# Four graph-attention layers on one core: the row factors G spread over the partitions by DMA and ScalarE in place of TensorE transposes

## The chip, the core and the metric

The kernel runs on one core of a Trainium2 chip. The metric is the device time of one launch in microseconds (us), the median of three runs. A core has a matrix engine (TensorE, in the profile PE for its matmuls and PEld for its weight loads), a vector engine (VectorE, DVE), a scalar engine (ScalarE, ACT), a general engine (GpSimd, POOL), and SyncE (SP), which here issues DMAs alone. The program emits one stream of instructions for each of them, and the streams wait for one another by semaphores. SBUF is the working memory, with 128 partitions; PSUM is the memory that the matmuls write to.

## The reference

Input: 16 graphs `x[b]` of 1024 nodes with 256 features, and one adjacency matrix `adj` (1024 x 1024) for all. Four layers run one after the other, each adding its result to `x`. Layers 0 and 2 have four heads of 64 features, layers 1 and 3 have one head of 256. Cut to what matters:

```
h = max(layernorm(x), 0)
q = h @ W                          # split into heads of D features
e[i,j] = leaky(a_src·q[i] + a_dst·q[j], slope)
e[i,j] = -inf where adj[i,j] == 0
x = x + act(softmax_j(e) @ q)      # act: elu in layers 0 to 2, relu in layer 3
```

Softmax is not changed by a factor that depends on i alone. The kernel uses this: up to such a factor, exp(leaky(s_i + d_j)) is exp(slope·d_j) times max(G_i, R_j), where G_i = exp(-(1-slope)·s_i) and R_j = exp((1-slope)·d_j), both with constants for safety. So the weight for head h is `w[j,i] = max(G[i], R[j]) * mask[j,i]`, with j on the partitions and i along the free axis. R is one number per partition. G varies along the free axis, so it has to stand as a row of 1024 numbers, the same in all 128 partitions. How it gets there is what the change is about.

## The kernel before

The work is cut into 64 **steps**, one for each pair of a graph and a layer. Four graphs (streams) are under way at a time, and the steps rotate over them (`order_of_steps`), so that a step's graph was last worked on four steps earlier in the steady part; in the first steps it is less. In the steady part four-head and one-head steps mostly alternate; steps 0 to 8 and the last three are irregular. The nodes are cut into C = 8 chunks of 128.

A step n has three parts.

**Preparation** (`preparation`, 17 pieces) gives layer norm statistics on VectorE (`bn`, L160; `mv`, L161), the reciprocal root on GpSimd (`rstd`, L164 and L165), the normalised tile `t` on GpSimd (L171, two halves of four instructions), transposes of it on TensorE (L179) that ScalarE takes out of PSUM with a relu (`hT`, L180), the projection on TensorE (L191) that ScalarE evacuates (`whx`, `sd`, L193 to L197), and last the `factors`: `rcol` (R, L203) and `gcol` (G, L206) on ScalarE, and a minimum on GpSimd (L208). `rcol` and `gcol` have a node on each partition. The PSUM tile `pp` (two buffers) serves transposes and projections.

**Aggregation** has 8 groups, k = 0 to 7. In a four-head step a head takes two groups, in a one-head step the head takes all eight. A group is a run of matmuls (`acc`, L243, two PSUM buffers) and one ScalarE evacuation (`y`, L247). Before it, `broadcast` (L217) makes the row G of a head in a PSUM tile `g` of 4 KB per partition (two buffers): eight TensorE transposes of a column of `gcol` that is repeated to 128 columns (L221). Then `weights` (L224) makes eight tiles `w` of 128 x 1024 on VectorE (L227); the tiles stand in a ring of `WBUFS` = 21 buffers.

**Finish** (`finish`) divides (`r`, L264; `y`, L268), takes the elu with GpSimd (L273), ScalarE (L274) and VectorE (L280), and adds into `x` on GpSimd (L281); in layer 3 it adds on VectorE (L283), stores with a DMA on SP (L284) and loads the next graph (L146).

The order in which everything is emitted is written out by hand, under `tc.manual_schedule()` (L349). For each group k of step n the loop emits: the `w` tiles that the group needs and that are still missing, the group's matmuls and its evacuation, pieces of the finish of step n-1 (at k = 0, 1, 2, 3), up to 4 (four heads) or 2 (one head) further `w` tiles with the `broadcast` that they need, and last the pieces of preparation that are due. The preparation of step n+2 is planned at group 0 of step n (for a few early steps and the last ones at group 4), and `PREPARATION` gives each piece's distance from there in groups: statistics at 0 and 1, `t` at 1, the first transposes at 3, the factors at 9. A `broadcast` can only be emitted once its step's last piece of preparation has been (`done["prepared"]`). In steps that are planned late, this makes the `broadcast` of the next step's first head come after group 6.

Of the kernel before, what the change touches and what calls it, by code (L numbers as in the profile page):

```python
# [24 lines left out]
F32 = mybir.dt.float32  # L25
# [3 lines left out]
AF = mybir.ActivationFunctionType  # L29
# [4 lines left out]
P = 128  # L34
# [1 line left out]
SHIFT = 60.0  # L36
EXP_SHIFT = math.exp(SHIFT)
STREAMS = 4
WBUFS = 21
PREPARATION = (0, 1, 1, 1, 3, 3, 4, 4, 5, 5, 6, 6, 7, 7, 8, 8, 9)  # L40


LAYERS = [
# [8 lines left out]
def kernel(ctx: ExitStack, tc: tile.TileContext, x, adj, ws, avs, out):  # L52
    nc = tc.nc
    B, N, F = x.shape
    C = N // P
# [5 lines left out]
    ident = const.tile([P, P], F32, name="ident")  # L61
# [17 lines left out]
    with tc.tile_pool(name="wprep", bufs=2) as wp, tc.tile_pool(  # L79
        name="wpsum", bufs=2, space=PSUM  # L80
    ) as wps:
        for l, (H, slope, hs, _) in enumerate(LAYERS):
# [3 lines left out]
            for part in range(2):  # L86
                nc.scalar.dma_start(
                    out=a_bc[:, part],
                    in_=bass.AP(tensor=avs[l].tensor, offset=avs[l].offset + part * D,
                                ap=[[0, P], [hs, H], [1, D]]),  # L90
# [24 lines left out]
    with tc.tile_pool(name="mprep", bufs=2) as mp, tc.tile_pool(  # L115
        name="mpsum", bufs=2, space=PSUM
# [16 lines left out]
    small = ctx.enter_context(tc.tile_pool(name="small", bufs=4))  # L133
    work = ctx.enter_context(tc.tile_pool(name="work", bufs=2))
    ps_g = ctx.enter_context(tc.tile_pool(name="ps_g", bufs=2, space=PSUM))
    ps_acc = ctx.enter_context(tc.tile_pool(name="ps_acc", bufs=2, space=PSUM))
    ps_p = ctx.enter_context(tc.tile_pool(name="ps_p", bufs=2, space=PSUM))

    L = len(LAYERS)
# [2 lines left out]
    state = [dict() for _ in steps]  # L142
# [5 lines left out]
    def preparation(n):  # L148

        b, l = steps[n]  # L150
        H, slope, _, _ = LAYERS[l]
        D = F // H
        st = state[n]

        def stats(half):
            if half == 0:
                st["mv"] = small.tile([P, C, 2], F32, name="mv")
                st["bn"] = small.tile([P, C, 6], F32, name="bn")
            for c in range(half * HALF, (half + 1) * HALF):
                nc.vector.bn_stats(st["bn"][:, c, :], xs[b][:, c, :])  # L160
                nc.vector.bn_aggr(st["mv"][:, c, :], st["bn"][:, c, :])  # L161
            if half == 1:
                rstd = st["rstd"] = small.tile([P, C], F32, name="rstd")
                nc.gpsimd.tensor_scalar(rstd, st["mv"][:, :, 1], EPS, None, op0=ALU.add)  # L164
                nc.gpsimd.tensor_tensor(rstd, rstd, neghalf, op=ALU.pow)  # L165

        def normalise(half):
            xn = st["xn", half] = prep.tile([P, HALF, F], F32, name="t4", bufs=3)
            for q in range(HALF):
                c = half * HALF + q  # L170
                nc.gpsimd.tensor_scalar(xn[:, q, :], xs[b][:, c, :], st["mv"][:, c, 0:1],  # L171
                                        st["rstd"][:, c:c + 1], op0=ALU.subtract, op1=ALU.mult)

        def transpose(half, k):
            if k == 0:
                st["hT", half] = prep.tile([P, K, HALF * P], F32, name="hT")
            pt = ps_p.tile([P, HALF, P], F32, name="pp")
            for q in range(HALF):
                nc.tensor.transpose(pt[:, q, :], st["xn", half][:, q, k * P:(k + 1) * P], ident)  # L179
            nc.scalar.activation(st["hT", half][:, k, :], pt.rearrange("p q i -> p (q i)"),  # L180
                                 AF.Relu)

        def project(c):
            if c == 0:
                st["whx"] = prep.tile([P, C, H, D + 1], F32, name="whx", bufs=3)
                st["sd"] = small.tile([P, C, 2 * H], F32, name="sd")
            whx = st["whx"]
            half, q = divmod(c, HALF)
            pw = ps_p.tile([P, F + 2 * H], F32, name="pp")
            for k in range(K):  # L190
                nc.tensor.matmul(pw, lhsT=st["hT", half][:, k, q * P:(q + 1) * P],  # L191
                                 rhs=wx[l][:, k, :], start=(k == 0), stop=(k == K - 1))
            nc.scalar.activation(whx[:, c, :, D], pw[:, F + H:F + 2 * H], AF.Exp, bias=nbias[l],  # L193
                                 scale=slope)
            nc.scalar.activation(st["sd"][:, c, :], pw[:, F:F + 2 * H], AF.Copy)
            for h in range(H):
                nc.scalar.activation(whx[:, c, h, 0:D], pw[:, h * D:(h + 1) * D], AF.Copy,  # L197
                                     scale=whx[:, c, h, D:D + 1])

        def factors():  # L200
            sd = st["sd"]
            rcol = st["rcol"] = small.tile([P, C, H], F32, name="rcol")
            nc.scalar.activation(rcol, sd[:, :, H:2 * H], AF.Exp, bias=rbias[l],  # L203
                                 scale=1.0 - slope)
            gcol = st["gcol"] = small.tile([P, C, H], F32, name="gcol")
            nc.scalar.activation(gcol, sd[:, :, 0:H], AF.Exp, bias=rbias[l],  # L206
                                 scale=-(1.0 - slope))
            nc.gpsimd.tensor_scalar(gcol, gcol, EXP_SHIFT, None, op0=ALU.min)  # L208

        out = [lambda: stats(0), lambda: stats(1), lambda: normalise(0), lambda: normalise(1)]  # L210
        for half in range(2):
            out += [lambda half=half, k=k: transpose(half, k) for k in range(K)]
            out += [lambda c=c: project(c) for c in range(half * HALF, (half + 1) * HALF)]

        return list(zip(PREPARATION, out + [factors], strict=True))

    def broadcast(n, h):  # L217

        g = state[n]["g", h] = ps_g.tile([P, N], F32, name="g")
        for c in range(C):  # L220
            nc.tensor.transpose(g[:, c * P:(c + 1) * P],  # L221
                                state[n]["gcol"][:, c, h:h + 1].to_broadcast([P, P]), ident)

    def weights(n, h, jc):  # L224

        w = state[n]["w", h, jc] = work.tile([P, N], F32, name="w", bufs=WBUFS)
        nc.vector.scalar_tensor_tensor(w, state[n]["g", h], state[n]["rcol"][:, jc, h:h + 1],  # L227
                                       masks[LAYERS[steps[n][1]][3]][:, jc, :],
                                       op0=ALU.max, op1=ALU.mult)
# [66 lines left out]
    def groups(n):  # L296
        if LAYERS[steps[n][1]][0] == 1:
# [3 lines left out]
    tiles = [(n, h, jc) for n, (b, l) in enumerate(steps) for h in range(LAYERS[l][0])  # L301
             for jc in range(C)]
    place = {t: i for i, t in enumerate(tiles)}
    done = {"tiles": 0, "g": 0, "free": 0, "prepared": 0, "wanted": 0}
    agenda = []

    def prepare(upto):

        while agenda and (agenda[0][0] <= upto or agenda[0][1] < done["wanted"]):
            _, n, piece, last = agenda.pop(0)  # L310
            piece()
            if last:
                done["prepared"] = n + 1

    def plan(n, at):
        new = preparation(n)
        agenda.extend((at + k, n, piece, i == len(new) - 1) for i, (k, piece) in enumerate(new))
        agenda.sort(key=lambda a: a[:2])

    def emit_tiles(upto, must=False):  # L320
        while done["tiles"] < min(upto, len(tiles)):
            i = done["tiles"]

            while done["g"] <= min(i + C // 2, len(tiles) - 1):
                n, h, _ = tiles[done["g"]]
                if n >= done["prepared"]:
                    if i < done["g"] or not must:
                        break
                    done["wanted"] = n + 1
                    prepare(-1)  # L330
                broadcast(n, h)
                done["g"] += C
            if i >= done["g"]:
                return
            weights(*tiles[i])
            done["tiles"] += 1
# [8 lines left out]
    for n in range(2):  # L345
        plan(n, -99)
        prepare(0)
    ending = []
    with tc.manual_schedule():  # L349
        for n in range(len(steps)):  # L350
            for k, (h, i0, per) in enumerate(groups(n)):
# [9 lines left out]
                ahead = 4 if per > 1 else 2  # L361
                emit_tiles(min(done["tiles"] + ahead, done["free"] + WBUFS))
                prepare(8 * n + k)
# [43 lines left out]
```

## Time and profile before

| what | value |
|---|---|
| runs | 2884.19, 2884.19, 2882.7 us; median 2884.19 |
| profiled execution, own time | 2886.49 us |
| its span, first to last instruction | 2884.7 us |
| mean granted TensorE clock | 0.986 |
| PE / DVE / ACT / POOL busy, share of the span | 94% / 69% / 33% / 48% |
| transposes that make G (L221) | 1280 of 277 ns, 171.9 us busy |
| `w` tiles (L227) | 1280 of 1271 ns, 1541.9 us busy |
| ScalarE, one 128 x 1024 pass (L274) | 96 of 1049 ns |
| DMA of 512 KB on SP, issue to landing | out 2.9 us, adjacency rows 3.6 us |

Busy time is the union of an engine's instructions; [...] 1280 transposes of 277 ns overlap to 171.9 us. A group's line in the profile gives the source line, the engine and operation, the output and inputs, the count, busy time and mean duration, and behind the second bar the engine's idle time just before these instructions and who ended it. A line of the timeline gives start and duration in us, and in square brackets the idle time before it.

### The profile page before, as it was taken

Reading aid. Unit: us, or ns where it says so; the run is one execution under the profiler, and the core shown is the slowest. Engines: PE = TensorE matmul, PEld = TensorE weight load, DVE = VectorE, ACT = ScalarE, POOL = GpSimd, SP = SyncE. Lnnn points to the kernel's source line nnn. Section 1 sums busy time; section 2 is a strip of 40 time slices with the busy share of each in tenths; the row PEclk is TensorE's granted clock in tenths of the full one; section 3 lists DMA queues with packets and bytes.
Section 4 is the critical chain, followed back from the end, with each engine's and each line's share of the span. In section 5 each row is a group of like instructions: output and inputs, shape, how many; then the busy total and the mean of one; then the engine's idle time right before and its main releaser. Section 6 shows DMA issues by size and latency. Waiting matters only on the chain.

```text
span 2884.7 us, 90415 instructions
## 1 busy us (share of the span) xinstructions
PE 2704.2 (94%) x41296; PEld 2408.5 (83%) x41296; DVE 1993.6 (69%) x2569; ACT 949.3 (33%) x3297; POOL 1384.1 (48%) x1037
## 2 busy tenths in 40 slices
PE   1899998999999999999999999999999999999998
PEld 1788887888988888888988888888888888888886
DVE  5697585576874687648867569667696477774673
ACT  0423423323323333333333333333333333333321
POOL 1445545445445456455355455455445445456342
PEclk9999999999999999999999999999999999999999
DMA  4000000000000000000000000000000000000000
GB/s 146 2 3 2 2 2 2 2 31 31 3 31 30 2 2 2 2 1 31 32 2 32 31 2 3 2 2 31 9 25 31 11 22 2 3 2 1 17 17 30
DMA packets 38845, 45.63 MB, mean 16 GB/s; under 512 B 3136, under 2 KB 37440, under 8 KB 38464
## 3 DMA queue, kind: packets, MB, share of 16 engines
q1 hardware_dynamic: 35776, 38.80, 4.0%
q8 instruction: 324, 5.31, 0.7%
q10 hardware_dynamic: 2688, 1.05, 0.1%
q14 instruction: 57, 0.47, 0.1%
HBM read 23.07 MB, written 16.78 MB: 14 GB/s over the span
## 4 chain that ended last, share of the span: by engine, by line
PE 63%; DVE 17%; POOL 16%; ACT 3%; issue 1%; DMA 1%; DVEq 0%; POOLq 0%; ACTq 0%
PE acc L243 43%; PE pp L191 13%; DVE w L227 12%; POOL t L171 11%; PE pp L179 3%; POOL rstd L165 3%; PE g L221 3%; DVE bn L160 2%; POOL rstd L164 1%; DVE mv L161 1%; ACT t L274 1%; ACT y L247 1%; DMA a_bc<-in_L_gnn_a 0%; DVE mask L129 0%; POOL gcol L208 0%
## 5 line engine op out<-in xcount | busy, mean ns | idle before, releaser
L243 PE MATMUL acc<-whx,w 128*64 128x65 f32 x36864 | 1971.2, 242 | 21.8 <-DVE w L227 21.7
L243 PEld LDWEIGHTS acc<-whx,w 128*64 128x64 f32 x36864 | 1770.1, 145 | 205.0 <-issue 48.0
L227 DVE SCALAR_TENSOR_TENSOR w<-g,rcol,mask 128x1024 f32<-128x1024 f32 x1280 | 1541.9, 1271 | 371.6 <-PE g L221 371.6
L247 ACT ACTIVATE y<-acc 128x260 f32<-128x260 f32 (+1 forms) x512 | 198.8, 388 | 1517.6 <-PE acc L243 1517.6
L171 POOL TENSOR_SCALAR t<-x,mv,rstd 128x256 f32<-128x256 f32 x512 | 650.4, 1285 | 61.1 <-PE pp L179 54.3
L268 POOL TENSOR_TENSOR y<-y,r 128x1024 f32<-128x1024 f32 x128 | 242.5, 1900 | 794.7 <-DVE r L264 794.7
L191 PE MATMUL pp<-wx,hT 128*128 128x258 f32 (+1 forms) x2048 | 505.3, 389 | 2.2 <-ACT whx L197 2.0
L191 PEld LDWEIGHTS pp<-wx,hT 128*128 128x128 f32 x2048 | 376.8, 190 | 65.3 <-ACT whx L197 7.1
L197 ACT ACTIVATE whx<-pp,whx 128x64 f32<-128x64 f32 (+1 forms) x1280 | 360.0, 348 | 0.0
L264 DVE RECIPROCAL r<-y 128x32 f32<-128x32 f32 (+1 forms) x64 | 17.7, 277 | 401.8 <-ACT y L247 401.8
L179 PE MATMUL pp<-ident,t 128*128 128x128 f32 x1024 | 160.9, 286 | 99.0 <-POOL t L171 95.6
L208 POOL TENSOR_SCALAR gcol<-gcol 128x32 f32<-128x32 f32 (+1 forms) x64 | 17.4, 272 | 453.5 <-ACT gcol L206 453.4
L281 POOL TENSOR_TENSOR x<-x,t 128x1024 f32<-128x1024 f32 x96 | 225.0, 2365 | 20.3 <-DVE t L280 20.3
L179 PEld LDWEIGHTS pp<-ident,t 128*128 128x128 f32 x1024 | 116.9, 142 | 133.1 <-POOL t L171 116.3
L160 DVE BATCH_NORM_STATS2 bn<-x 128x6 f32<-128x256 f32 x512 | 202.5, 396 | 2.5 <-DMA x<-in_x 2.5
L180 ACT ACTIVATE hT<-pp 128x512 f32<-128x512 f32 x256 | 140.3, 595 | 182.2 <-PE pp L179 180.8
L193 ACT ACTIVATE whx<-pp,nbias 128x4 f32<-128x4 f32 (+1 forms) x512 | 137.2, 268 | 189.7 <-PE pp L191 177.0
L221 PE MATMUL g<-ident,gcol 128*128 128x128 f32 x1280 | 171.9, 277 | 0.5 <-POOL gcol L208 0.5
L280 DVE SCALAR_TENSOR_TENSOR t<-t,y 128x1024 f32<-128x1024 f32 x96 | 123.6, 1288 | 64.5 <-ACT t L274 64.5
L221 PEld LDWEIGHTS g<-ident,gcol 128*128 128x128 f32 x1280 | 139.9, 136 | 14.1 <-POOL gcol L208 0.7
L165 POOL TENSOR_TENSOR rstd<-rstd,neghalf 128x8 f32<-128x8 f32 x64 | 107.7, 1682 | 5.3
L273 POOL TENSOR_SCALAR t<-y 128x1024 f32<-128x1024 f32 x96 | 103.4, 1077 | 9.0
(31 smaller groups left out, 468.5 us busy)
## 6 DMA issues: line engine op xcount, KB each, us to landing
x<-in_x SPq DMA_DIRECT2D x16, 1024.0 KB, 5.4
out<-x SPq DMA_DIRECT2D x32, 512.0 KB, 2.9
a_raw<-in_adj SPq DMA_DIRECT2D x8, 512.0 KB, 3.6
a_bc<-in_L_gnn_a ACTq DMA_DIRECT2D x8, 128.0 KB, 5.9
wx<-in_L_gnn_W SPq DMA_DIRECT2D x4, 256.0 KB, 12.3
```

What stands on the lines that cost most here:

```text
L160: nc.vector.bn_stats(st["bn"][:, c, :], xs[b][:, c, :])
L165: nc.gpsimd.tensor_tensor(rstd, rstd, neghalf, op=ALU.pow)
L171: nc.gpsimd.tensor_scalar(xn[:, q, :], xs[b][:, c, :], st["mv"][:, c, 0:1], st["rstd"][:, c:c + 1], op0=ALU.subtract, op1=ALU.mult)
L179: nc.tensor.transpose(pt[:, q, :], st["xn", half][:, q, k * P:(k + 1) * P], ident)
L191: nc.tensor.matmul(pw, lhsT=st["hT", half][:, k, q * P:(q + 1) * P], rhs=wx[l][:, k, :], start=(k == 0), stop=(k == K - 1))
L197: nc.scalar.activation(whx[:, c, h, 0:D], pw[:, h * D:(h + 1) * D], AF.Copy, scale=whx[:, c, h, D:D + 1])
L221: nc.tensor.transpose(g[:, c * P:(c + 1) * P], state[n]["gcol"][:, c, h:h + 1].to_broadcast([P, P]), ident)
L227: nc.vector.scalar_tensor_tensor(w, state[n]["g", h], state[n]["rcol"][:, jc, h:h + 1], masks[LAYERS[steps[n][1]][3]][:, jc, :], op0=ALU.m ...
L243: nc.tensor.matmul(acc[o % P:o % P + cols, q, :], lhsT=st["w", h, jc][:, o:o + cols], rhs=st["whx"][:, jc, h, :], start=(jc == 0), stop=(j ...
L247: nc.scalar.activation(st["y"][:, i0:i0 + per, h, :], acc, AF.Copy)
L268: nc.gpsimd.tensor_tensor(yh, yh, r[:, :, None].to_broadcast([P, HALF * H, D]), op=ALU.mult)
L281: nc.gpsimd.tensor_add(xh, xh, e)
```

## The change

G is no longer made by TensorE. A new last piece of preparation, `rows`, transposes the whole of `gcol` (all heads and chunks) once on TensorE, copies it from PSUM to an SBUF tile `gT` on ScalarE, and stores it from SP to a DRAM tile `grow`. For each head, `fetch` loads the row of 1024 numbers from DRAM into all partitions of an SBUF tile `gs` (two buffers, a DMA of 512 KB on SP). `broadcast` is then one ScalarE copy of `gs` into the PSUM tile `g`. A fetch is emitted up to two heads ahead of the copies (`fetch_heads`), once the step's preparation has been emitted.

`rows` is due one group after the factors, and it is now the last piece of preparation, so a step counts as prepared one group later. `WBUFS` goes from 21 to 19, which frees 8 KB per partition; the two buffers of `gs` take 8 KB.

```
-WBUFS = 21
-PREPARATION = (0, 1, 1, 1, 3, 3, 4, 4, 5, 5, 6, 6, 7, 7, 8, 8, 9)
+WBUFS = 19
+PREPARATION = (0, 1, 1, 1, 3, 3, 4, 4, 5, 5, 6, 6, 7, 7, 8, 8, 9, 10)
...
+    dram = ctx.enter_context(tc.tile_pool(name="dram", bufs=4, space=bass.MemoryType.DRAM))
...
+        def rows():
+
+            pt = ps_p.tile([C * H, P], F32, name="pp")
+            nc.tensor.transpose(pt, st["gcol"].rearrange("p c h -> p (c h)"), ident)
+            gT = small.tile([C * H, P], F32, name="gT", bufs=2)
+            nc.scalar.activation(gT, pt, AF.Copy)
+            st["grow"] = dram.tile([H, C, P], F32, name="grow")
+            nc.sync.dma_start(out=st["grow"].rearrange("h c i -> c h i"), in_=gT)
...
-        return list(zip(PREPARATION, out + [factors], strict=True))
+        return list(zip(PREPARATION, out + [factors, rows], strict=True))
+
+    def fetch(n, h):
+
+        gs = state[n]["gs", h] = work.tile([P, N], F32, name="gs", bufs=2)
+        nc.sync.dma_start(out=gs, in_=state[n]["grow"][h].rearrange("c i -> (c i)")
+                          .partition_broadcast(P))
 
     def broadcast(n, h):
 
         g = state[n]["g", h] = ps_g.tile([P, N], F32, name="g")
-        for c in range(C):
-            nc.tensor.transpose(g[:, c * P:(c + 1) * P],
-                                state[n]["gcol"][:, c, h:h + 1].to_broadcast([P, P]), ident)
+        nc.scalar.activation(g, state[n]["gs", h], AF.Copy)
...
             if last:
                 done["prepared"] = n + 1
+                fetch_heads()
...
+    def fetch_heads():
+
+        while done["gs"] < min(done["g"] + 2 * C, len(tiles)):
+            n, h, _ = tiles[done["gs"]]
+            if n >= done["prepared"]:
+                break
+            fetch(n, h)
+            done["gs"] += C
...
                 broadcast(n, h)
                 done["g"] += C
+                fetch_heads()
```

More of the change, by code (lines that the diff above doesn't have):

```diff
@@ L303 @@
     place = {t: i for i, t in enumerate(tiles)}
-    done = {"tiles": 0, "g": 0, "free": 0, "prepared": 0, "wanted": 0}
+    done = {"tiles": 0, "g": 0, "gs": 0, "free": 0, "prepared": 0, "wanted": 0}
     agenda = []
```

## The prediction

> **What bounds the kernel now.** I read the page, then the waits of a steady stretch (1000 to 2000 us), then the timeline of one pair of steps (24 and 25), then busy time and clock in short windows.
>
> ```profile
> PE 2704.2 (94%) x41296; PEld 2408.5 (83%) x41296; DVE 1993.6 (69%) x2569; ACT 949.3 (33%) x3297; POOL 1384.1 (48%) x1037
> PE 63%; DVE 17%; POOL 16%; ACT 3%; issue 1%; DMA 1%; DVEq 0%; POOLq 0%; ACTq 0%
> L221 PE MATMUL g<-ident,gcol 128*128 128x128 f32 x1280 | 171.9, 277 | 0.5 <-POOL gcol L208 0.5
> ```
>
> TensorE is nearly always busy, and the transposes of G are 6% of that. But the chain that ended last leaves TensorE for a third of its length. The waits say where:
>
> ```profile
> DVE w L227 <- PE g L221: 101.6, 23, 9.0
> PEld pp L179 <- POOL t L171: 40.2, 35, 1.6
> PE pp L179 <- POOL t L171: 33.3, 31, 1.4
> ```
>
> In the steady part TensorE waits for one thing, the normalised tile `t`, once per step. Step 24 (four heads), PE alone:
>
> ```profile
> 1174.17 1.09 PE L221 MATMUL g<-ident,gcol 128*128 128x128 f32 x8
> 1184.55 1.09 PE L221 MATMUL g<-ident,gcol 128*128 128x128 f32 x8
> 1189.45 0.67 PE L179 MATMUL pp<-ident,t 128*128 128x128 f32 x3
> 1191.29 0.77 PE L179 MATMUL pp<-ident,t 128*128 128x128 f32 x5 [1.17 <-POOL t L171]
> 1195.87 1.09 PE L221 MATMUL g<-ident,gcol 128*128 128x128 f32 x8
> ```
>
> Two broadcasts lie **before** the wait for `t`, one after. What sets `t`? In step 24: the last `y` of the step before, `r` on DVE at 1169.07, eight `w` and eight `bn`/`mv` pairs, `rstd`, then four `t` that end at 1191.24. In step 25 (one head) it hangs on group 1's `y`: ACT, then POOL:
>
> ```profile
> 1225.42 0.29 ACT L206 ACTIVATE gcol<-sd,rbias 128x8 f32<-128x8 f32 x1
> 1225.79 0.25 POOL L208 TENSOR_SCALAR gcol<-gcol 128x8 f32<-128x8 f32 x1 [5.52 <-ACT gcol L206]
> 1226.45 1.67 POOL L165 TENSOR_TENSOR rstd<-rstd,neghalf 128x8 f32<-128x8 f32 x1
> 1228.22 5.15 POOL L171 TENSOR_SCALAR t<-x,mv,rstd 128x256 f32<-128x256 f32 x4
> ```
>
> Neither chain contains a broadcast. The broadcast of step 25 at 1227.07 lies beside the second one, and PE still waits 1.17 us at its end. So TensorE time removed between a chain's start and its `t` becomes a longer wait, and only what is removed between `t` and the step's end shortens the step.
>
> **What a wait costs besides.** Four windows, busy time of PE and granted clock:
>
> ```profile
> 1144.72:1148.13 3.41, 1.46 (x10) 1.20 (x10) 3.41 (x4) 0.97 (x3) 2.42 (x3) 1.00 0.00 0
> 1148.13:1151.54 3.41, 3.41 (x10) 2.67 (x9) 3.41 (x4) 0.33 (x1) 3.41 (x3) 0.50 0.00 0
> 1189.09:1192.50 3.41, 2.24 (x40) 1.67 (x36) 3.41 (x4) 1.24 (x3) 2.42 (x3) 1.00 0.00 0
> 1192.50:1195.91 3.41, 3.41 (x119) 3.34 (x115) 3.41 (x4) 0.24 (x1) 3.41 (x4) 1.00 0.02 5
> ```
>
> With 1.95 us idle in one such window the next runs at half clock (matmuls of 635 ns instead of 380); with 1.17 it doesn't. The half-clock stretches all fit one grid of 3.41 us. On it, idle of 1.89 us or more in a window was always followed by half clock, 1.38 or less never, 1.6 to 1.7 sometimes.
>
> [...] the trace has 2.9 us (store of 512 KB) and 3.6 (load of 512 KB). [...] In step 23, with L280 amid the four `t`, they took 5.93 us against 5.15.
>
> **The change part by part**, against the profiled span of 2884.7 us (own time 2886.5; the median of the runs, 2884.2, is 0.5 below the span).
>
> *Removed:* 160 broadcasts. One holds TensorE's weight stream 0.92 us on average (start of its first load to the next other load: 0.82 to 1.02), 147 us in all. From the emission loop I place them in the steady part, steps 9 to 60 (25 four-head, 27 one-head). Before `t`: heads 2 and 3 of each four-head step, and the next step's head 0 in one-head steps: nothing won. After `t`: in 19 four-head steps with a one-head step next, one of 0.82; in 6 with a four-head step next, two, of which DVE, busy with `w` until the end, lets about 0.8 through; in 20 one-head steps before a four-head step, one of 0.98. Sum 15.6 + 4.8 + 19.6 = **-40 us**. In steps 0 to 8 and 61 some 22 broadcasts have no such wait behind them, but VectorE is close: half of 20, **-10**.
>
> *Moved:* in one-head steps DVE no longer takes `w` ahead of the second L280, so that runs before `t` instead of within it: 0.78 us in each of the 16 steps with the 5.93 form, **-13** (bounds 0 and -13).
>
> *Half clock.* In four-head steps PE comes to `t` 1.84 us earlier, less 0.4 for the one transpose of `rows` (0.14 each for L179's, and a change of shape of up to 0.34): idle 1.17 becomes some 2.7, spread over 3.2 us. Depending on how the grid falls, about 0.65 of the 25 exceed 1.65 us in one window; at half clock 3.41 us lose 1.7, of which some falls into the wait: 1.5. **+24**. One-head steps: all 27 get about 1.95 us, what the 16 had of which 13 tripped: 0.8 x 27 - 13 = 8.6 more at 1.7, **+15**. Bounds 0 and +70.
>
> *First heads that come late.* For steps 3, 5, 6, 8, 62 and 63 the factors come at group 5 and the broadcast after group 6; the end shows what then follows:
>
> ```profile
> 2837.70 1.03 PE L221 MATMUL g<-ident,gcol 128*128 128x128 f32 x8
> 2838.86 9.62 DVE L227 SCALAR_TENSOR_TENSOR w<-g,rcol,mask 128x1024 f32<-128x1024 f32 x8 [19.84 <-PE g L221]
> 2848.53 0.70 PE L243 MATMUL acc<-whx,w 128*128 128x257 f32 x2 [0.49 <-DVE w L227]
> ```
>
> The last `w` gates PE, and `w` starts 1.3 us after group 6. Now after group 6: transpose, `y` (0.39), `gT` (about 0.3) = 0.9; the store of `grow` (16 KB or less[...]); the load of `gs` (512 KB: 3.3, between 2.9 and 3.6; the smaller broadcast load `a_bc` took 2.9 at its best, so repeated reading isn't slow); SP's two issues about 0.4; the ScalarE copy 1.05 by L274 of the same size (two halves like L180 would be 1.19). Sum 7.7, +0.1 to start: 6.5 later, six times, **+39**. At the start, where the two first preparations still run beside it, **+4**. Stalls this long bring a half-clock window each, five new: **+8**.
>
> *Costs nothing:* 160 copies on ScalarE (168 us) lie under its waits for `acc` (1517.6 us). Behind a copy wait `whx` and `hT`, which PE needs a group later. In one-head steps the copy comes one group after `rows`: `gs` lands 10.1 us after group 1's end, the copy ends at 11.2, `hT` at 12.3, and PE asks for it at 13.4: 1.1 us to spare, no more. SP's waits for L283 (its stores) come ahead of a fetch only in steps after layer 3, with two groups to spare. Two `w` buffers fewer: the limit of 19 isn't reached in the steady loop, but the later readiness leaves a lead of 2 and 6 tiles at four-head groups instead of 4 and 8. By DVE's order the last `w` of group 4 is ready 0.2 us before PE asks; if not, up to 1 us in 25 steps.
>
> Sum: -40 -10 -13 +24 +15 +39 +4 +8 = **+27**: span 2912, median **2912 us**.
>
> **Rivals.**
> *The clock isn't tripped oftener* (against: the trace's 1.89 us; for: the wait is split by transposes): without +24, +15 and +8, 2912 - 47 = **2865**, faster. It decides at about 20 new half-clock windows less: with some 12 instead of 30 the balance is zero.
> *The round trip through DRAM takes 8 us instead of 5.7:* one-head steps lose 2.3 - 1.1 = 1.2 x 27 = 32, the late heads 2.3 x 7 = 16: **2960**. For: loads among others took up to 5.4 us (1 MB); against: DMA engines are near idle.
> *TensorE is the bound throughout:* -147, + 64 x 0.4 for `rows`: **2763**. For: 94% busy. Against: the wait for `t` in every steady step.
> *The broadcast load from one DRAM row is slow* (10 us and more): ScalarE stands in every one-head step, over **3000**.
>
> **How the numbers follow.** Likeliest case 0.60 (2890 to 2935); no new half clock 0.15; slow round trip 0.14; TensorE throughout 0.03; slow broadcast 0.03; near zero, between the first two, 0.05. About 0.2% (5.8 us) is what a measurement can tell from no change: faster 0.16, same 0.07, slower 0.77. The range from 2860 to 2965 takes in the first three and leaves out about 0.15.
>
> **What would show it.** Right: L179's wait for `t` grows to about 2.7 us in four-head and 1.9 in one-head steps; half-clock stretches rise from 19 (the one at the very end apart) to over 40 and the mean clock falls from 0.986 to about 0.97; the six first heads start their `w` some 6 us later, with DVE waiting for ACT; four-head steps of 44.8 us stay within 1 us. Wrong: PE's idle time unchanged and the span down by over 100; or `hT` late behind the copy, with ScalarE waiting for `gs` in the steady part.

## The result, and the profile after

The changed kernel takes 2913.1 us (median of four runs, 2904.8 to 2916.8), against 2883.4 for the kernel before on the same chip: a ratio of 1.010, 95% interval 1.0075 to 1.0125. Each experiment further down ran beside the kernel before again, whose median was then 2880.3 us (b_onetr, b_late, a_fill, a_late9), 2884.7 (b_tr4, a_tr4, a_fill9, b_fill) or 2878.9 (the last four): the ratios are against these, the differences against the 2883.4 and 2913.1 above. The profiled execution has a span of 2907.9 us (own time 2909.8) and a mean granted clock of 0.964; before it was 2884.7 and 0.986.

From the page of the kernel after: the engines, the chain that ended last by engine, and three groups of instructions. The last line, for comparison with L180, is from the page of the kernel before.

```profile
PE 2642.2 (91%) x40080; PEld 2315.1 (80%) x40080; DVE 1992.7 (69%) x2569; ACT 1095.9 (38%) x3521; POOL 1376.2 (47%) x1037
PE 59%; DVE 18%; POOL 16%; ACT 3%; DMA 2%; issue 2%; DVEq 0%; SPq 0%; POOLq 0%; ACTq 0%
L192 PE MATMUL pp<-wx,hT 128*128 128x258 f32 (+1 forms) x2048 | 513.5, 393 | 3.6 <-ACT whx L198 2.6
L180 PE MATMUL pp<-ident,t 128*128 128x128 f32 x1024 | 183.0, 296 | 153.6 <-POOL t L172 150.0
L236 ACT ACTIVATE g<-gs 128x1024 f32<-128x1024 f32 x160 | 163.8, 1024 | 70.8 <-DMA gs<-grow 70.8
L179 PE MATMUL pp<-ident,t 128*128 128x128 f32 x1024 | 160.9, 286 | 99.0 <-POOL t L171 95.6
```

The 1280 transposes and their 171.9 us are gone, yet PE's busy time fell by 62 us only: the `acc` matmuls take 42 us more than the 1971.2 they took before, the same 36864 matmuls of 245 ns after 242 at the lower clock, L180 takes 22 more than its 160.9, and `rows` has 17.5. In the whole record PE now stands 150 us waiting for `t`, where it was 95.6. The copies of G on ScalarE (L236) are there, 1.02 us each, and the projections behind them (L192) hardly wait: 3.6 us in all.

The waits of the steady stretch, 1000 to 2000 us (total, times, longest):

```profile
DVE w L241 <- ACT g L236: 113.8, 17, 15.0
PE pp L180 <- POOL t L172: 52.6, 70, 1.2
ACT g L236 <- DMA gs<-grow: 27.6, 12, 3.1
```

The same wait as before, for the same tile, went from 33.3 us to 52.6. Step 24 on PE shows its form:

```profile
1207.58 0.27 PE L214 MATMUL pp<-ident,gcol 128*8 128x128 f32 x1
1211.67 0.33 PE L180 MATMUL pp<-ident,t 128*128 128x128 f32 x1
1212.43 0.33 PE L180 MATMUL pp<-ident,t 128*128 128x128 f32 x1 [0.43 <-POOL t L172]
1213.63 0.33 PE L180 MATMUL pp<-ident,t 128*128 128x128 f32 x1 [0.87 <-POOL t L172]
1215.12 0.77 PE L180 MATMUL pp<-ident,t 128*128 128x128 f32 x5 [1.17 <-POOL t L172]
```

PE now comes early enough to wait for three of the four `t`: 0.43 + 0.87 + 1.17 = 2.47 us where it was 1.17. Two windows of the clock's grid around it (columns: length, busy time of PE, PEld, DVE, ACT, POOL, then the granted clock):

```profile
1212.90:1216.31 3.41, 1.51 (x22) 1.16 (x24) 3.41 (x4) 0.82 (x2) 2.41 (x3) 1.00 0.30 94
1216.31:1219.73 3.42, 3.42 (x71) 3.42 (x67) 3.42 (x4) 0.27 (x1) 3.42 (x4) 0.50 0.02 5
```

1.90 us idle in the first, and the next runs at half clock. The border that the prediction read from the kernel before (1.89 us or more always, 1.38 or less never) is less sharp in the other traces of this case: there, from the first `acc` on, full-clock windows with 1.4 to 2.0 us of idle time (in the kernel after 1.47 to 1.75) were sometimes followed by half clock and sometimes not, those with more than 2.02 us always. Steady four-head steps did not do this before at all. Steady steps 9 to 60, each counted from its first `acc` matmul to the next step's and sorted by whether a half-clock stretch begins in them (step 60, which borders on the irregular end, is left out of the one-head rows):

| steady steps | before | after |
|---|---|---|
| four-head, full clock | 25 of 45.08 us | 9 of 44.03 |
| four-head, half clock | none | 16 of 45.92 |
| one-head, full clock | 13 of 39.7 | 14 of 39.1 |
| one-head, half clock | 13 of 42.5 | 12 of 41.2 |

By part of the span (the start up to the first `acc`, and steps 61 to 63 up to the end of the last one), with the half-clock stretches of the whole record and of steps 9 to 59. Parts and stretches are those of one profiled execution, the median is that of all runs; the experiments' rows are read further down:

| kernel | median us | first `acc` | steps 0 to 8 | steps 9 to 60 | steps 61 to 63 | half clock, all / steady |
|---|---|---|---|---|---|---|
| before | 2883.4 | 99.0 | 426.6 | 2232.2 | 115.7 | 20 / 13 |
| after | 2913.1 | 102.2 | 456.0 | 2213.0 | 125.6 | 42 / 28 |
| b_onetr | 2840.7 | 94.9 | 416.5 | 2204.7 | 112.4 | 33 / 26 |
| b_late | 2885.1 | 101.7 | 444.1 | 2202.1 | 122.3 | 11 / 0 |
| a_fill | 2870.6 | 103.8 | 459.0 | 2171.3 | 126.0 | 14 / 1 |
| a_late9 | 2894.9 | 105.3 | 443.3 | 2213.4 | 123.0 | 44 / 29 |
| a_fill9 | 2847.9 | 103.4 | 441.1 | 2173.2 | 119.8 | 13 / 3 |
| b_fill | 2862.4 | 101.3 | 424.0 | 2209.5 | 114.9 | 7 / 0 |
| b_tr4 | 2811.3 | 101.3 | 442.2 | 2137.8 | 117.9 | 11 / 0 |
| a_tr4 | 2913.2 | 105.1 | 476.9 | 2187.1 | 133.9 | 39 / 22 |
| b_tr4_19 | 2813.4 | 99.5 | 441.8 | 2138.4 | 120.8 | 9 / 0 |
| a_tr4_g1 | 2909.2 | 104.7 | 468.7 | 2187.4 | 133.8 | 39 / 21 |
| a_tr4_r9 | 2906.6 | 104.7 | 480.8 | 2186.7 | 130.2 | 40 / 21 |
| a_tr4_g1r9 | 2901.7 | 105.3 | 477.8 | 2185.6 | 128.8 | 40 / 19 |

The change's +23 us of span are +3 at the start, +29 in steps 0 to 8, **-19** in the steady steps, +10 at the end. The end once more, on the path to step 63's first `w` in the kernel after:

```profile
2855.26 0.27 PE L214 MATMUL pp<-ident,gcol 128*8 128x128 f32 x1
2855.74 0.25 ACT L216 ACTIVATE gT<-pp 8x128 f32<-8x128 f32 x1
2856.01 0.28 SPq L218 DMA_DIRECT2D grow<-gT  x1
2857.28 0.33 SPq L230 DMA_DIRECT2D gs<-grow  x1
2860.97 1.03 ACT L236 ACTIVATE g<-gs 128x1024 f32<-128x1024 f32 x1 [1.54 <-DMA gs<-grow]
2862.03 9.63 DVE L241 SCALAR_TENSOR_TENSOR w<-g,rcol,mask 128x1024 f32<-128x1024 f32 x8 [26.71 <-ACT g L236]
2863.37 16.87 PE L257 MATMUL acc<-whx,w 128*128 128x257 f32 x52 [4.36 <-DVE w L241]
```

From TensorE's first instruction on G to the first `w` it is 6.77 us. In the kernel before, the same two instructions stand at 2837.70 and 2838.86, 1.16 us apart. Over the six late first heads, the first `w` starts 5.4 to 7.4 us later after group 6 than it did, 6.1 on average.

### The profile page after: what moved, and what is told of

The parts are those of the page before. It is cut to its first block, busy times and chain, and to the rows that moved or that the text cites. A ratio compares the mean times of both kernels' runs of the same rounds, so it can differ in the third digit from the quotient of the medians.

```text
span 2907.9 us, 89029 instructions
## 1 busy us (share of the span) xinstructions
PE 2642.2 (91%) x40080; PEld 2315.1 (80%) x40080; DVE 1992.7 (69%) x2569; ACT 1095.9 (38%) x3521; POOL 1376.2 (47%) x1037
## 4 chain that ended last, share of the span: by engine, by line
PE 59%; DVE 18%; POOL 16%; ACT 3%; DMA 2%; issue 2%; DVEq 0%; SPq 0%; POOLq 0%; ACTq 0%
PE acc L257 42%; DVE w L241 12%; PE pp L192 12%; POOL t L172 10%; PE pp L180 4%; POOL rstd L166 3%; DVE bn L161 3%; DVE mv L162 1%; POOL rstd L165 1%; DMA gs<-grow 1%; ACT t L288 1%; POOL gcol L209 1%; ACT y L261 1%; DMA a_bc<-in_L_gnn_a 0%; ACT g L236 0%
## 5 line engine op out<-in xcount | busy, mean ns | idle before, releaser
L257 PE MATMUL acc<-whx,w 128*64 128x65 f32 x36864 | 2013.5, 245 | 47.0 <-DVE w L241 47.0
L257 PEld LDWEIGHTS acc<-whx,w 128*64 128x64 f32 x36864 | 1800.0, 148 | 248.0 <-DVE w L241 70.9
L172 POOL TENSOR_SCALAR t<-x,mv,rstd 128x256 f32<-128x256 f32 x512 | 627.2, 1237 | 65.0 <-PE pp L180 58.2
L192 PE MATMUL pp<-wx,hT 128*128 128x258 f32 (+1 forms) x2048 | 513.5, 393 | 3.6 <-ACT whx L198 2.6
L192 PEld LDWEIGHTS pp<-wx,hT 128*128 128x128 f32 x2048 | 380.0, 191 | 73.6 <-ACT whx L198 7.8
L180 PE MATMUL pp<-ident,t 128*128 128x128 f32 x1024 | 183.0, 296 | 153.6 <-POOL t L172 150.0
L180 PEld LDWEIGHTS pp<-ident,t 128*128 128x128 f32 x1024 | 121.3, 144 | 204.0 <-POOL t L172 189.6
L209 POOL TENSOR_SCALAR gcol<-gcol 128x32 f32<-128x32 f32 (+1 forms) x64 | 33.3, 520 | 436.0 <-ACT gcol L207 435.9
L294 DVE SCALAR_TENSOR_TENSOR t<-t,y 128x1024 f32<-128x1024 f32 x96 | 121.8, 1268 | 164.5 <-ACT t L288 164.4
L236 ACT ACTIVATE g<-gs 128x1024 f32<-128x1024 f32 x160 | 163.8, 1024 | 70.8 <-DMA gs<-grow 70.8
L165 POOL TENSOR_SCALAR rstd<-mv 128x8 f32<-128x8 f32 x64 | 39.1, 610 | 156.8 <-DVE mv L162 154.5
```

The source lines that it names most:

```text
L236: nc.scalar.activation(g, state[n]["gs", h], AF.Copy)
L257: nc.tensor.matmul(acc[o % P:o % P + cols, q, :], lhsT=st["w", h, jc][:, o:o + cols], rhs=st["whx"][:, jc, h, :], start=(jc == 0), stop=(j ...
```

## The experiments

My theory: TensorE time taken away ahead of the wait for `t` only lengthens that wait, the longer wait trips the clock, and the steps whose first G comes late pay for the way through DRAM. The first rival: TensorE is the bound throughout, and something else in the change (the copies, the loads) eats the 147 us. The second: the clock plays no part.

**b_onetr**: the kernel before with one of the eight transposes of a G, so seven eighths of what the change takes from TensorE are taken and nothing is added. The rest of the row isn't made: two fixed PSUM tiles, filled once at the start, stand in for `g` by turns.

```
-        g = state[n]["g", h] = ps_g.tile([P, N], F32, name="g")
-        for c in range(C):
+        g = state[n]["g", h] = held[len(heads) % 2]
+        heads.append(h)
+        for c in range(1):
```

> The kernel before with one of a head's eight transposes of G, the other seven chunks of G left as they were set once at the start (so seven eighths of G is left out); no DMA, no copy, no later readiness. It frees about 0.75 us of TensorE per head, 120 us in all. My theory (only what is freed after t shortens a step, and longer waits for t trip the clock): -35 after t, -9 in the first steps, +35 to +40 from half clock: 2870 to 2890 us, L179's waits for t up to about 2.5 us in four-head steps, and 35 to 42 half-clock stretches instead of 19. Rival, TensorE is the bound throughout: about 2764 us. Rival, the clock is not tripped oftener: about 2840 us.

Measured: 2840.7 us, ratio 0.986 (0.9835 to 0.988). Its waits for `t`, 1000 to 2000 us:

```profile
PE pp L185 <- POOL t L177: 49.8, 57, 1.4
```

They are near those of the kernel after (52.6), without any copy, store or load, and the steady half-clock stretches double from 13 to 26. So **TensorE isn't the bound**: nearly 130 us of it (1120 transposes, 7/8 of the 147 us of the prediction) brought some 40. My 2870 to 2890 missed too. The 2840.7 is the very figure of the last rival in the expectation, that the clock isn't tripped oftener, but the doubled stretches speak against it: taken alone, the time would have misled. 13 more stretches came in the record where I had counted on 16 to 23, and the one-head steps gained besides: the first four `t` take 5.3 us or less in nearly all of them, where 16 had 5.93. Why they do was not isolated.

**b_late**: the other half of the change alone. G stays on TensorE, but the kernel before gets an empty last piece of preparation at 10 and 19 buffers.

```
-WBUFS = 21
-PREPARATION = (..., 8, 8, 9)
+WBUFS = 19
+PREPARATION = (..., 8, 8, 9, 10)
...
-        return list(zip(PREPARATION, out + [factors], strict=True))
+        return list(zip(PREPARATION, out + [factors, lambda: None], strict=True))
```

> The kernel before with 19 w buffers and an empty last piece of preparation at distance 10, so that a step counts as prepared one group later; G stays with TensorE. My theory: the six late first heads (steps 3, 5, 6, 8, 62, 63) start their w one group later, 3.5 to 5.8 us each, 30 in all, a half-clock stretch each (+5): about 2915 us (2905 to 2925), with the steady steps 9 to 60 unchanged within 10 us. Rival, the late heads lie beside other work: 2884. Rival, the shorter lead of w (2 and 6 tiles instead of 4 and 8) stalls TensorE in the four-head steps: up to 25 us more, about 2940, with waits for w in the steady part.

Measured: 2885.1 us, 1.001 (0.9998 to 1.002). The sum is as the rival had it, but made of two large terms. The first heads that come late do cost (+17.5 in steps 0 to 8, +6.6 at the end). No matmul wait of the four-head steps came of the shorter lead: they take 45.07 us after 45.08. The steady steps win 30, of which the 13 half-clock stretches that are gone are 22 by the measure of b_fill below: in one-head steps the next G's transposes, and DVE's `w`, move behind the second L280. G then fills TensorE's time right before the wait for `t`, and L280 no longer falls amid the four `t`: the wait is 1.45 to 1.50 us in nearly all of these steps, where 13 of them had 1.96. From 1000 to 2000 us:

```profile
PE pp L179 <- POOL t L171: 29.4, 34, 1.2
```

So each half of the change alone wins some 30 us in the steady steps (27.5 for b_onetr); together they win 19. In b_late the transposes of G stand where part of the wait would be, and none of these steps trips the clock; in the kernel after they are gone, the wait is 1.97 to 2.03 us again, and 12 of them do.

**a_fill**: the kernel after, with useless work ahead of the wait: 4 or 8 matmuls of the identity with itself into the PSUM tile that the transposes overwrite.

```
             pt = ps_p.tile([P, HALF, P], F32, name="pp")
+            if half == 0 and k == 0:
+                for _ in range(8 if LAYERS[steps[max(n - 2, 0)][1]][0] > 1 else 4):
+                    nc.tensor.matmul(pt[:, 0, :], lhsT=ident, rhs=ident, start=True, stop=True)
```

> The kernel after with extra matmuls of the identity ahead of a preparation's first transposes, into the tile that these overwrite: eight in four-head steps (about 1.7 us of TensorE), four in one-head steps (0.9 us). They add about 80 us of TensorE work and nothing else. My theory: they lie within the wait for t, keep the clock's windows busy, and half-clock stretches fall from 41 to 20 or 25: about 2885 us, faster than the kernel after by 20 to 35. Rival, half clock has nothing to do with the time: same, 2913. Rival, TensorE is the bound: about 2990.

Measured: 2870.6 us, 0.997 (0.995 to 0.998) of the kernel before, so 42 us less than the kernel after (38 by the ratios). Step 24 on PE (L217 is `rows`, L183 the transposes of `t`):

```profile
1200.86 0.27 PE L217 MATMUL pp<-ident,gcol 128*8 128x128 f32 x1
1204.95 2.05 PE L181 MATMUL pp<-ident 128*128 128x128 f32 x16
1206.83 0.49 PE L183 MATMUL pp<-ident,t 128*128 128x128 f32 x3
1208.42 0.77 PE L183 MATMUL pp<-ident,t 128*128 128x128 f32 x5 [1.09 <-POOL t L172]
```

The matmuls take the place of the wait: what was 2.47 us of idle time is 1.09. The steady part loses 27 of its 28 half-clock stretches and 41.7 us, 1.5 us for each. The gain lies in the steps that had such a stretch and in no others, compared step by step:

| steady steps, median change of a step | had a half-clock stretch | had none |
|---|---|---|
| one-head, after to a_fill | 12 of -1.66 us | 14 of +0.02 |
| four-head, after to a_fill | 15 of -1.55 | 9 of +0.02 |
| one-head, before to b_fill (below) | 13 of -1.68 | 13 of -0.01 |

**That the clock plays no part is refuted**: TensorE was given more to do, and the kernel became faster. The kernel before says the same without an edit: of the 39 runs beside this one, those with a granted clock of 0.985 took 2888.8 us on average, those with 0.990 2876.1.

**a_late9**: the kernel after, with `rows` at 9 instead of 10, but only in steps that are planned at group 4.

```
         new = preparation(n)
+        if at % 8 == 4:
+            new[-1] = (9, new[-1][1])
```

> The kernel after with the piece rows at distance 9 instead of 10 in those steps alone that are planned at group 4 (the late first heads). The store and load through DRAM then start a group earlier. My theory: each late first head starts its w 3 to 4 us earlier (the round trip of about 5 us after gT then sets it, no longer a group and the round trip), six times: about 2892 us (2886 to 2900), steady steps unchanged. Rival, the late heads cost nothing: 2913.

Measured: 2894.9 us, 1.004 (1.003 to 1.006): 12.7 less in steps 0 to 8, 2.6 less at the end, the steady part unchanged; the start took 3.1 more. Some 15 us of the cost of the late first heads lie in those steps, as said, but at the end only 2.6 of the 9.9 us came back.

**a_fill9** has both of these edits, and **b_fill** the matmuls of a_fill in the kernel before, ahead of the wait in one-head steps only (`range(4)`, under the condition `LAYERS[...][0] == 1`).

> The kernel after with identity matmuls ahead of the first transposes (2870.6 alone, 42 us less) and the rows of G one group earlier in the steps that are planned late (2894.9 alone, 16 to 18 us less). The two act in different steps (the steady ones, and the first nine and the last), so they should add: 2852 us. If late steps and clock are one and the same loss, no less than 2868 us.

> The kernel before with four identity matmuls ahead of the first transposes of a step prepared during a one-head step. Its 13 half-clock stretches in the steady steps follow those waits for t of 1.96 us. [...] 13 x 1.7 us = 22 us go: 2860 us, with at most 3 half-clock stretches in the steady steps. If the kernel before does not lose by its clock, 2880 us or a little more, by the added matmuls.

Measured: a_fill9 2847.9 us, 0.988 (0.986 to 0.990); b_fill 2862.4, 0.993 (0.991 to 0.995). The two losses add, and the clock's share in the kernel before is 22.7 us in the steady steps, 1.68 in each step that had one of the 13 stretches. Half of a stretch of 3.41 us is 1.7. The kernel with G through DRAM is now the faster one: 14 us ahead of b_fill.

**b_tr4 and a_tr4** plan the first transposes one group later, past the end of the chain to `t`, in the kernel before and after. Only the transposes of the first half of the nodes move, and the first two projections with them; those of the second half stay, though the expectation of b_tr4 speaks of each half.

```
-PREPARATION = (0, 1, 1, 1, 3, 3, 4, 4, 5, 5, ...
+PREPARATION = (0, 1, 1, 1, 4, 4, 5, 5, 5, 5, ...
```

> The kernel before, with the first two transposes of each half planned one row group later (PREPARATION 4, 4, 5, 5, 5, 5 in place of 3, 3, 4, 4, 5, 5): by then t is done. If the waits for t and the half-clock stretches that follow them are the whole loss of the steady steps, some 60 of the 75 us of idle TensorE and the 13 half-clock stretches (worth about 22 us) go: about 2800 us, half-clock stretches below 10. If the wait is only handed on (transposes that come closer together wait for ScalarE to empty their PSUM bank, or the next t starts later), no less than 2860 us.

> The kernel after with the same one group later. If the change's steady steps are held up by the wait for t and by the clock, and not by TensorE, DVE or the broadcast, 120 us of idle TensorE and about 28 half-clock stretches go: 2775 to 2810 us, and it is then faster than the same edit of the kernel before by the 40 us of TensorE work that the change removes, less its slower first and last steps (about 45 us slower): within 15 us of it. If DVE (about 43 us of work in a four-head step) or the copy of G on ScalarE then binds, 2830 us or more, with waits for w in the steady steps.

Measured: b_tr4 2811.3 us, 0.975 (0.973 to 0.977), the fastest of all these kernels (94 us less in the steady steps, 16 more in steps 0 to 8); a_tr4 2913.2, 1.011 (1.009 to 1.013), **over 100 us more than I expected**. The chain that ended last, b_tr4:

```profile
PE 86%; DVE 7%; POOL 3%; ACT 2%; DMA 1%; issue 1%; SPq 0%; DVEq 0%; ACTq 0%; POOLq 0%
```

The bound is TensorE now, and in its steady one-head and four-head steps (38.5 and 43.9 us) PE idles for 11 us in all. The same for a_tr4, and two of its waits from 1000 to 2000 us:

```profile
PE 63%; DVE 26%; ACT 4%; issue 3%; POOL 2%; DMA 2%; DVEq 0%; ACTq 0%; POOLq 0%; SPq 0%
```

```profile
DVE w L241 <- ACT g L236: 105.8, 12, 15.0
PE acc L257 <- DVE w L241: 40.1, 36, 2.1
```

The wait for `t` is gone here too (16.4 us in the whole record), and one-head steps take 37.4 us, 1.2 less than in b_tr4. But in four-head steps PE waits in group 4 for `w` of the third head, in 22 of the 25 a half-clock stretch begins amid or right after these waits, and they take 47.1. Counting finished `w` tiles, DVE is 10 tiles ahead as such a step starts, and 12 in b_tr4 (the expectation below has 13); as its group 4 starts, mostly 21 of the 24 tiles asked for are done, and 24 in b_tr4. Either the two buffers fewer or G's later arrival in the one-head step before takes this lead. Three runs for that:

**b_tr4_19**: b_tr4 with `WBUFS = 19`. **a_tr4_g1**: a_tr4 with one buffer of `gs` and `WBUFS = 20`. **a_tr4_r9**: a_tr4 with `rows` at 9 in all steps. A fourth, **a_tr4_g1r9**, joins the last two.

> The kernel before with the transposes one group later (2811 alone) and 19 buffers of w in place of 21. At the start of a four-head step DVE is 13 tiles of w ahead with 21 buffers and 10 with the changed kernel's 19. If the lost buffers are what stops the changed kernel from gaining by the later transposes, each of the 25 steady four-head steps loses up to two tiles of 1.2 us, less what slack there is: 2840 to 2875 us, with waits of the matmuls for w in group 4 of these steps. If it is G that comes late, and not the buffers, 2811 to 2820 us.

> The kernel after with later transposes (2913 alone), one buffer of gs in place of two and 20 of w in place of 19. If buffers decide, DVE is one tile further ahead in each steady four-head step: 25 x 1.2 us = 30 us less, 2875 to 2890 us. If G's round trip decides, or the single gs makes a load wait for the copy ahead of it, 2913 us or more.

> The kernel after with later transposes (2913 alone) and the rows of G one group earlier, right after their factors, in all steps. If G's lateness costs the other tile of the lead (10 where the buffers would let 11), the steady four-head steps win up to 1.2 us each (30 us); the steps that are planned late win about 16 us as they did with the transposes where they were: 2870 us. If buffers alone decide in the steady steps, only the 16 us: 2897 us. TensorE's wait for gcol at the rows may take some of either back (up to 1 us a step).

> Both of these edits of the kernel after with later transposes: lead 12 in place of 10, rows earlier. If DVE's lead in the four-head steps is what holds it, the gains add: 2913 - 30 - 43 = 2840 us; 2865 us if rows give their 16 us only. If neither is the cause, 2897 us or more.

Measured: 2813.4, 2909.2, 2906.6 and 2901.7 us; ratios 0.975 (0.973 to 0.977), 1.009 (1.0065 to 1.011), 1.008 (1.0045 to 1.011), 1.007 (1.004 to 1.009). **The buffers are not it**: two fewer cost b_tr4 some 2 us at most and leave its lead at 12 in 19 of 25 steps, 11 in the others; one more, with one `gs` less, doesn't change a_tr4's lead of 10. G's arrival is: with `rows` one group earlier the lead is 12 in nearly all steps, and steady four-head steps fall from 47.1 to 44.0 us. I had expected a faster kernel of that; it isn't, because one-head steps rise from 37.4 to 40.3. What PE waits for there, a_tr4_r9 from 1000 to 2000 us, and where, in step 17:

```profile
PE pp L214 <- POOL gcol L209: 48.6, 24, 2.2
```

```profile
937.46 0.25 POOL L209 TENSOR_SCALAR gcol<-gcol 128x8 f32<-128x8 f32 x1 [5.51 <-ACT gcol L207]
937.76 0.27 PE L214 MATMUL pp<-ident,gcol 128*8 128x128 f32 x1 [2.13 <-POOL gcol L209]
```

`rows` is now emitted right behind the factors, and TensorE stands 2.1 us for `gcol`, long enough for the clock again: of the 21 half-clock stretches in steps 9 to 59, 20 begin within 1.5 us of the end of such a wait. One wait is put in place of another. A place for `rows` between the two, or one that TensorE reaches with other work in hand, wasn't tried.

## Why the prediction was right

The median of 2913.1 against the 2912 predicted is closer than the terms are, and part of that is luck. The four runs go from 2904.8 to 2916.8; the profiled spans differ by 23 us where +27 was the sum; and two terms of the one-head steps missed by 13 and 18 us in opposite directions (point 3). By its own steps:

1. *What bounds the kernel*: right. The wait for `t` once a step holds both kernels; b_tr4, whose edit only moves the first transposes, removes it and wins 72 us. In the kernel after the same edit wins nothing, since the wait for `w` takes its place.
2. *Removed, -40 in the steady part, and the clock in four-head steps, +24*: the mechanism right, and both sizes too. The two rows of the table hold different steps, so their means don't give a price; a_fill runs 24 of the same 25 steps at full clock. Against it the kernel before takes 19 us more in these steps, where 20 was counted, and the kernel after 23 more, where 24 was. The share that trips was put at 0.65 of 25, which is 16, and it was 16, mostly at 1.55 us each (1.5 was counted).
3. *One-head steps*: this is where terms failed. The -13 for L280 counted what `t` gains and not where L280 goes: the four `t` fell even further, to 4.84 us, but L280 (now L294) meets the GpSimd instruction on `gcol` (L209), whose mean went from 272 to 520 ns. In 24 of these 27 steps it takes 0.90 us or a little more, where it took 0.25 to 0.30. Step 25 in the kernel after (before: 0.25, in the prediction's lines):

```profile
1249.95 1.23 DVE L294 SCALAR_TENSOR_TENSOR t<-t,y 128x1024 f32<-128x1024 f32 x1 [4.00 <-ACT t L288]
1250.38 0.90 POOL L209 TENSOR_SCALAR gcol<-gcol 128x8 f32<-128x8 f32 x1 [5.53 <-ACT gcol L207]
```

That instruction stands ahead of `rstd` and `t` in the same queue, so up to 0.65 us a step is given back. Its mean is 517 ns in b_late too, which has no DMA of G. And the +15 for the clock did not come: half-clock stretches in one-head steps are 12 after 13, though nearly all these steps now wait 1.97 to 2.03 us (forecast 1.9). The idle time now stands in three pieces over some 3 us, between single transposes; that a grid window therefore catches less of it fits the record, but no run isolates it. Together the one-head steps went from 40.9 to 40.1 us, 27 x 0.86 = -23, where -19.6 - 13 + 15 = -18 was counted. With a_fill and b_fill as these steps at full clock, the -23 are -20 (counted: -32.6) and, for the clock, 19 us after 22: -3 (counted: +15).
4. *Late first heads, +39, start +4, clock there +8, early steps -10*: measured +29 in steps 0 to 8, +10 at the end and +3 at the start, 42 against 41 in sum. The +8 can't be told apart: half-clock time in steps 0 to 8 and 61 to 63, the stretch at the very end left out, rises from 24 to 89 us, much more than five windows, but part of it lies within the stalls themselves. Of the way through DRAM the store was over-sized (its share of the 7.7 us was my estimate, and no trace of the kernel before shows such a store): from the end of `gT` to the copy it is 5.0 us, not 5.7; SP issues the load 1.27 us after the store, and the copy starts 3.7 us after that. The delay of step 63's `w` is 6.77 - 1.16 = 5.6 us, not 6.5; the six average 6.1. a_late9 shows where part of the cost lies, and b_late that 24 us of it would be there with G on TensorE.
5. *What costs nothing*: right. ScalarE does wait for `gs` in every steady one-head step, 1.3 to 3.1 us (70.8 in the whole record), which the prediction had named, with a late `hT`, as a sign of being wrong; but `hT` isn't late, and no projection of a steady step waits (3.6 us in all, outside these steps); two buffers fewer cost next to nothing (b_tr4_19). The cover is the wait for `t`: with that gone, in a_tr4, G's later arrival shows as 3.2 us in each four-head step against b_tr4.
6. *The rivals*: TensorE as the bound is refuted by b_onetr, the slow round trip by the 5.0 us, the slow broadcast load by its 3.7. "No added half clock" was named at 2865 us and is refuted by the 28 steady stretches after 13. The 2870.6 of a_fill isn't that rival's case, as it also takes away the 13 stretches that the kernel before had.

A half-clock stretch of 3.41 us cost 1.66 to 1.68 us in one-head steps and mostly 1.55 in four-head steps. The prediction's signs of being right all stood: wait for `t` 2.5 us (forecast 2.7), clock 0.964 (0.97), 41 half-clock stretches besides the one at the end (over 40), four-head steps of 45.24 us on average (44.8 within 1), the six first heads 6.1 us later (some 6).

## What to carry to other kernels

Of nearly 130 us of work taken off the busiest engine in b_onetr, some 40 showed in the time: find what ends the engine's last wait and on which side of it the work stands, before counting its time. A wait of TensorE of just under 2 us had a second price in the clock here, so either move the consumer past it (72 us here, for one row of planning distances) or give the engine something to do (some 40 and 22 us here). And a longer way for an operand (here 5.6 us through DRAM) can be free behind one stall and become the next bound when that stall is mended: test it with the stall gone.

## What the hardware showed that I had not expected

- Matmuls that compute nothing made both kernels faster, by some 40 us (104 us of such work on TensorE in a_fill) and by 22 us, and only in the steps that had run at half clock.
- A store of 4 KB to DRAM and a load that depends on it were issued by SP 1.27 us apart; the 512 KB load from one row to 128 partitions was in use 3.7 us later.
- An instruction of 128 x 8 elements on GpSimd took 0.90 us beside a 128 x 1024 one of VectorE (L294), and 0.25 us alone: in proportion it suffered more than the four `t` did (5.93 us with such an instruction among them, 4.84 without).
